# Two layers of a graph network on one core: layer 0 issued in rounds written out by hand, over four tiles at different stages

## Chip, cores and metric

The kernel runs on one core of a Trainium2 chip. The metric is device time in microseconds (us), median of the runs shown. A core has TensorE (PE; its weight loads, PEld, are listed apart), VectorE (DVE), ScalarE (ACT), GpSimd (POOL) and SyncE (SP). All DMAs of this kernel are issued from SP's queue. ACT evaluates its functions from tables that are loaded in sets by an instruction of its own (ACT_TABLE_LOAD).

## The reference

3327 nodes, 128 features, a dense 0/1 adjacency matrix. Layer 0 is attention by cosine, layer 1 attention with eight channels in each of 128 slices, both with a residual and a layer norm.

```python
# layer 0
norm2 = jnp.linalg.norm(x, axis=1, keepdims=True)
cos = beta[0] * (x @ x.T) / (norm2 @ norm2.T + 1e-07)
masked = cos + (1.0 - adj) * -1000000000.0
P = jax.nn.softmax(masked, axis=1)
x = _layernorm(x + P @ x)
# layer 1
q = (x @ Wq.T).reshape(d, n, h)          # k, v alike; d = 128, h = 8
a = jnp.einsum('dnh,dmh->dnm', q, k) * scale
a = a + adj + adj
a = jax.nn.softmax(a, axis=2)
out = jnp.einsum('dnm,dmh->dnh', a, v).reshape(n, h * d)
x = _layernorm(x + out @ Wo.T)
```

## The kernel before, in words

The nodes are padded to 3328 = 26 tiles of 128. Four stages follow one another: layer 0 (with the projections to q, k and v), a pass over DRAM that turns q and k and lays out v, the attention of layer 1, and the last projection with its layer norm.

**Layer 0** takes the tiles one by one in a loop over t. Tile t holds the nodes p*26+t, one on each partition p. For each tile:

- `load_adj` brings 128 rows of the adjacency matrix into `raw` (1.66 MB), two buffers.
- `turn_adj` turns these rows on PE, four blocks of 128x128 at a time into the PSUM tile `tp` (two buffers, seven chunks), and ACT copies them as bf16 into `aT` (L242). Three tiles share one `aT`, which goes to DRAM for layer 1.
- `inverse` gives 1/(norm_q*norm_k+1e-7): on ACT a logarithm (L252) and an exponential of its negative (L253), on POOL the denominator (L255) and its product with that first value (L258), on DVE one Newton step (L259). The product goes into the buffer `s`, of which there are two, and which the scores then use.
- `scores0`: POOL turns `raw` into the mask (L264); in four pieces of 832 columns PE makes the products and DVE scales them (L267), adds the mask and keeps the minimum (L270); ACT takes the exponential and its sum (L281).
- `values0` turns these weights on PE, copies each chunk to SBUF (`pt`, on DVE and ACT by turns, L155 and L153), multiplies by x (L291), and normalises (L295 to L312): the root is exp(-0.5*ln(var)) on ACT (L306, L307), refined on DVE (L309 to L311).
- `project` turns the new row block x1 (L318) and multiplies by the three weight matrices in halves of 512 columns (L326); the copies out are on DVE and ACT (L328, L155, L153), and a DMA takes each row block to DRAM.

x1 stays in SBUF until the last stage. In this stage the order on each engine is the scheduler's: the text gives loop order, and the scheduler moves instructions within what the data allow. The call that loads the common table set for exp and log (L232) is an instruction like the others.

**The attention stage** is issued by hand: inside `tc.manual_schedule` the order on PE, ACT, DVE and POOL is that of the text. It goes over blocks of three tiles and 32 units a block, 26 steps a unit. `load_adj_tile` (L443) brings a piece of the turned adjacency for the next block, and `exp_adj_tile` takes its exponential five steps later.

**The last stage** loads the outputs row block by row block, turns and projects them, adds x1 (L823) and normalises.

Of the kernel before, what the change touches and what calls it, by code (L numbers as in the profile page):

```python
# [10 lines left out]
F32 = mybir.dt.float32  # L11
# [35 lines left out]
def gnn_two_layers(  # L47
# [24 lines left out]
    x1 = const.tile([P, T, D], F32, name="x1")  # L72
# [11 lines left out]
    aT_s = dram.tile([NB, P, T, QT * P], BF16, name="aT_s")  # L84
# [86 lines left out]

    with ExitStack() as l0:
        big = l0.enter_context(tc.tile_pool(name="l0_big", bufs=1))
        adj_raw = l0.enter_context(tc.tile_pool(name="adj_raw", bufs=2))
        adj_tp = l0.enter_context(tc.tile_pool(name="adj_tp", bufs=1))
        work = l0.enter_context(tc.tile_pool(name="l0_work", bufs=2))
        ptp = l0.enter_context(tc.tile_pool(name="l0_pt", bufs=3))
        ps_sc = l0.enter_context(tc.tile_pool(name="l0_sc", bufs=2, space=PSUM))
        ps_tp = l0.enter_context(tc.tile_pool(name="l0_tp", bufs=2, space=PSUM))
        ps_x = l0.enter_context(tc.tile_pool(name="l0_x", bufs=2, space=PSUM))  # L180

        xs = big.tile([P, T, D], F32, name="xs")
        nc.gpsimd.memset(xs[:, T - 1, :], 0.0)
        xf = xs.rearrange("p t d -> p (t d)")
        for part, width in node_parts():
            nc.sync.dma_start(xf[part, :width], node_blocks(x, part, width))
        nbeta = const.tile([P, 1], F32, name="nbeta")
        nc.sync.dma_start(nbeta, bass.AP(tensor=beta.tensor, offset=beta.offset, ap=[[0, P], [1, 1]]))
        nc.vector.tensor_scalar_mul(nbeta, nbeta, -1.0)
        ones = const.tile([P, P], F32, name="ones")  # L190
        nc.gpsimd.memset(ones, 1.0)

        tiny = const.tile([P, 1], F32, name="tiny")
        nc.gpsimd.memset(tiny, 1e-7 * 2.0**-20)
        back = const.tile([P, 1], F32, name="back")
        nc.gpsimd.memset(back, -20.0 * math.log(2.0))

        raws = {0: load_adj(adj_raw, 0)}
        ws = []
        for name, w in (("wq", wqT), ("wk", wkT), ("wv", wvT)):  # L200
            wt = big.tile([P, C], F32, name=name)
            nc.sync.dma_start(wt, w)
            ws.append(wt)

        xT = big.tile([P, NP], F32, name="xT")
        for c in range(NCH):
            tp, a, b = turn(ps_tp, lambda t: xs[:, t, :], c)
            copy(c, xT.rearrange("r (p t) -> r t p", t=T)[:, a:b, :], tp)


        sq = work.tile([P, NP], F32, name="s")
        nc.gpsimd.tensor_mul(sq, xf, xf)
        norm_q = const.tile([P, T], F32, name="norm_q")
        nc.vector.reduce_sum(norm_q, sq.rearrange("p (t d) -> p t d", t=T), axis=AX.X)
        nc.scalar.activation(norm_q, norm_q, AF.Sqrt)
        norm_s = const.tile([P, T], F32, name="norm_s")
        nc.vector.tensor_scalar_mul(norm_s, norm_q, 2.0**-20)
        sqT = work.tile([P, NP], F32, name="s")
        nc.vector.tensor_mul(sqT, xT, xT)
        norm_k = big.tile([P, NP], F32, name="norm_k")  # L220
# [9 lines left out]
        for j in range(NPC):  # L230
            nc.scalar.activation(piece(norm_k, j), score_piece(ones, sqT, j), AF.Sqrt)
        nc.scalar.preload_act_table_set("natural_log_exp_and_others")  # L232

        def turn_adj(t: int, raw):

            b, i = divmod(t, QT)
            if i == 0:
                turn_adj.aT = adj_tp.tile([P, T, QT * P], BF16, name="aT")
            aT = turn_adj.aT
            for c in range(NCH):  # L240
                tp, k0, k1 = turn(ps_tp, lambda k: every(raw, k), c)
                nc.scalar.copy(aT[:, k0:k1, i * P : (i + 1) * P], tp)  # L242
            if i == QT - 1:
                nc.sync.dma_start(aT_s[b], aT)
            elif t == T - 1:
                w = (i + 1) * P
                nc.sync.dma_start(aT_s[b][:, :, :w], aT[:, :, :w])

        def inverse(t: int):

            y = work.tile([P, NP], F32, name="y")
            nc.scalar.activation(y, norm_k, AF.Ln, bias=tiny, scale=norm_s[:, t : t + 1])  # L252
            nc.scalar.activation(y, y, AF.Exp, bias=back, scale=-1.0)  # L253
            s = work.tile([P, NP], F32, name="s")
            nc.gpsimd.tensor_scalar(  # L255
                s, norm_k, norm_q[:, t : t + 1], 1e-7, op0=ALU.mult, op1=ALU.add
            )
            nc.gpsimd.tensor_mul(s, s, y)  # L258
            nc.vector.scalar_tensor_tensor(y, s, -2.0, y, op0=ALU.add, op1=ALU.mult)  # L259
            return s, y  # L260

        def scores0(t: int, raw, s, y):
            mn = small.tile([P, NPC], F32, name="mn")
            nc.gpsimd.tensor_scalar(raw, raw, -1.0, 1.0e9, op0=ALU.add, op1=ALU.mult)  # L264
            for j in range(NPC):
                sc = score_piece(every(xT, t), xT, j)
                nc.vector.scalar_tensor_tensor(  # L267
                    piece(s, j), sc, nbeta, piece(y, j), op0=ALU.mult, op1=ALU.mult
                )
                nc.vector.tensor_tensor_reduce(  # L270
                    out=piece(s, j),
                    in0=piece(s, j),
                    in1=piece(raw, j),
                    scale=-1.0,
                    scalar=BIG if j == 0 else mn[:, j - 1 : j],
                    op0=ALU.add,
                    op1=ALU.min,
                    accum_out=mn[:, j : j + 1],
                )
            den = small.tile([P, 1], F32, name="den0")  # L280
            nc.scalar.activation(s, s, AF.Exp, bias=mn[:, NPC - 1 : NPC], scale=-1.0, accum_out=den)  # L281
            return den

        def values0(t: int, s, den):
            acc = ps_x.tile([P, 512], F32, name="px")[:, :D]
            for c in range(NCH):
                tp, k0, k1 = turn(ps_tp, lambda k: every(s, k), c)
                pt = ptp.tile([P, 4, P], F32, name="pt")[:, : k1 - k0, :]
                copy(c, pt, tp)
                for k in range(k0, k1):  # L290
                    nc.tensor.matmul(  # L291
                        acc, pt[:, k - k0, :], xs[:, k, :], start=(k == 0), stop=(k == T - 1)
                    )
            rden = small.tile([P, 1], F32, name="rden0")
            nc.vector.reciprocal(rden, den)  # L295
            hid = small.tile([P, D], F32, name="hid")
            nc.vector.scalar_tensor_tensor(hid, acc, rden, xs[:, t, :], op0=ALU.mult, op1=ALU.add)

            stats = small.tile([P, nc.vector.BN_STATS_DIM], F32, name="stats0")
            mv = small.tile([P, nc.vector.BN_AGGR_DIM], F32, name="mv0")  # L300
            nc.vector.bn_stats(stats, hid)
            nc.vector.bn_aggr(mv, stats)
            var = small.tile([P, 1], F32, name="var0")
            nc.vector.tensor_scalar(var, mv[:, 1:2], EPS, None, op0=ALU.add)
            r = small.tile([P, 1], F32, name="r0")
            nc.scalar.activation(r, var, AF.Ln)  # L306
            nc.scalar.activation(r, r, AF.Exp, scale=-0.5)  # L307
            u = small.tile([P, 1], F32, name="u0")
            nc.vector.scalar_tensor_tensor(u, r, var, r, op0=ALU.mult, op1=ALU.mult)  # L309
            nc.vector.tensor_scalar(u, u, -0.5, 1.5, op0=ALU.mult, op1=ALU.add)  # L310
            nc.vector.tensor_mul(r, r, u)  # L311
            nc.vector.tensor_scalar(  # L312
                x1[:, t, :], hid, mv[:, 0:1], r, op0=ALU.subtract, op1=ALU.mult
            )

        def project(t: int):
            tp = ps_x.tile([P, 512], F32, name="px")
            nc.tensor.transpose(tp[:, :P], x1[:, t, :], ident)  # L318
            x1T = ptp.tile([P, P], F32, name="x1T")
            nc.scalar.copy(x1T, tp[:, :P])  # L320
            for n, (wt, dst) in enumerate(zip(ws, (q_s, k_s, v_s))):
                row = ptp.tile([P, C], F32, name="row")
                for i in range(2):
                    pq = ps_x.tile([P, 512], F32, name="px")
                    half = slice(i * 512, (i + 1) * 512)
                    nc.tensor.matmul(pq, x1T, wt[:, half], start=True, stop=True)  # L326
                    if n == 0:
                        nc.vector.tensor_scalar_mul(row[:, half], pq, float(D) ** -0.5)  # L328
                    else:
                        copy(i, row[:, half], pq)  # L330
# [536 lines left out]
```

## Time and profile before

| What | us |
|---|---|
| Median of 3 runs | 16244.1 (16243.56 to 16246.24) |
| The profiled execution | 16240.19 |
| Its span, first to last instruction | 16238.4 |
| PE busy in the span | 15584.8 (96%) |
| DVE busy | 13924.8 (86%) |
| ACT busy | 12722.5 (78%) |
| POOL busy | 13962.9 (86%) |

The profile is of one execution. "Busy" counts time in which an engine has an instruction in work; a row of the groups reads line, engine, operation, output<-inputs with shapes, count, then busy us, mean ns of one, and the idle time before them with what ended it. In the timeline the columns are start, duration, engine, line, operation, and in brackets the idle time before it and its releaser. The granted PE clock is a share of the full clock. TensorE's fp32 matmuls appear as two records each, its transposes as one.

### The profile page before, as it was taken

To read this page: it belongs to the slowest core of one execution; us is meant where nothing else is said; L and a number is where in the kernel's file an instruction comes from. 1 tells how busy PE (TensorE), PEld (TensorE's weight loads), DVE (VectorE), ACT (ScalarE), POOL (GpSimd) and SP (SyncE) were. 2 spreads that over 40 slices of the span, in tenths; PEclk is the share of its full clock that TensorE was granted. 3 is DMA by queue.
4 is the path that set the end of the run, shared out by engine and by line. 5 is a ranking of instruction groups with operands and counts; after the bars stand their busy time and mean duration, and the time that the engine had idled before them with its cause. 6 is when DMAs were issued, how large, how long until landed. Compare 5 with 4: busy or idle time off the path is not lost.

```text
span 16238.4 us, 506936 instructions
## 1 busy us (share of the span) xinstructions
PE 15584.8 (96%) x217532; PEld 7003.8 (43%) x217532; DVE 13924.8 (86%) x16184; ACT 12722.5 (78%) x24850; POOL 13962.9 (86%) x9107
## 2 busy tenths in 40 slices
PE   6765999999999999999999999999999999999999
PEld 5542444444444444444444444444444444444555
DVE  5545999999999999999999999999999999998775
ACT  5533888888888888888888888888888888888776
POOL 3334999999999999999999999999999999998886
PEclk7776999999999999999999999999999999999999
DMA  2245111111111111111111111111111111111112
GB/s 101 100 169 213 50 44 50 56 50 48 46 56 50 50 46 53 51 50 50 44 56 50 50 50 51 50 50 50 55 46 50 50 56 46 48 50 59 60 60 70
DMA packets 415024, 988.90 MB, mean 61 GB/s; under 512 B 192224, under 2 KB 312544, under 8 KB 367200
## 3 DMA queue, kind: packets, MB, share of 16 engines
q1 hardware_dynamic: 412768, 956.46, 17.1%
q8 instruction: 1704, 27.92, 0.7%
q14 instruction: 552, 4.52, 0.1%
HBM read 808.05 MB, written 148.24 MB: 59 GB/s over the span
## 4 chain that ended last, share of the span: by engine, by line
PE 89%; DVE 2%; issue 0%; ACT 0%; DMA 0%; SPq 0%; POOL 0%; ACTq 0%; POOLq 0%; DVEq 0%
PE acc L625 28%; PE ea L595 20%; PE m L516 15%; PE eb L608 12%; PE ea L608 9%; PE ea L614 2%; PE eb L614 2%; DVE mx L531 1%; PE ea L581 1%; PE ea L643 1%; DVE mx L552 1%; PE pp L822 0%; ACT pa L770 0%; DVE oT L155 0%; DMA vt_s<-vals 0%
## 5 line engine op out<-in xcount | busy, mean ns | idle before, releaser
L741 POOL TENSOR_TENSOR pb<-pb,eT 128x768 f32<-128x768 f32 (+1 forms) x7488 | 13182.9, 1766 | 1090.6 <-ACT pb L740 815.4
L531 DVE TENSOR_REDUCE mx<-m 128x2 f32<-128x1024 f32 x6784 | 8277.8, 1220 | 512.4 <-PE eb L614 214.0
L740 ACT ACTIVATE pb<-eb 128x768 f32<-128x768 f32 (+1 forms) x7488 | 5901.6, 788 | 2498.1 <-PE eb L614 1639.2
L516 PE MATMUL m<-kx,qx 32*128 32x512 f32 (+1 forms) x23296 | 6767.6, 470 | 71.6 <-DVE mx L531 40.2
L770 ACT ACTIVATE pa<-ea 128x384 f32<-128x384 f32 (+1 forms) x14976 | 6336.2, 477 | 51.0 <-PE ea L595 38.9
L625 PE MATMUL acc<-pb,vt 128*9 128x384 f32 (+1 forms) x29952 | 5903.1, 474 | 0.1
L625 PE MATMUL acc<-pa,vt 128*9 128x384 f32 (+1 forms) x29952 | 5900.3, 474 | 0.0
L552 DVE TENSOR_REDUCE mx<-m 128x1 f32<-128x512 f32 x6400 | 4382.6, 685 | 682.4 <-PE m L516 317.9
L608 PEld LDWEIGHTS <-one 3*128 3x128 bf16 x29952 | 1519.0, 91 | 5537.6 <-issue 4656.5
L595 PE MATMUL ea<-aT,two 128*32 128x384 bf16 (+1 forms) x59904 | 3715.0, 325 | 0.0
L614 PE MATMUL ea<-qx,kx 32*128 32x384 f32 (+1 forms) x14976 | 3458.8, 437 | 0.0
L614 PE MATMUL eb<-qx,kx 32*128 32x384 f32 (+1 forms) x14976 | 3443.1, 451 | 0.0
L608 PE MATMUL ea<-cx,one 3*128 3x384 bf16 (+1 forms) x14976 | 3309.0, 322 | 1.2
L516 PEld LDWEIGHTS m<-kx,qx 32*128 32x128 f32 x23296 | 2814.7, 182 | 453.4 <-DVE mx L531 95.4
L608 PE MATMUL eb<-cx,one 3*128 3x384 bf16 (+1 forms) x14976 | 2464.1, 326 | 9.7 <-ACT pb L740 8.9
L625 PEld LDWEIGHTS acc<-pa,vt 128*9 128x9 f32 x29952 | 1410.4, 91 | 788.5 <-issue 0.3
L595 PEld LDWEIGHTS <-two 128*32 128x32 bf16 x59904 | 945.5, 95 | 1418.6 <-issue 1278.1
L614 PEld LDWEIGHTS eb<-qx,kx 32*128 32x128 f32 x14976 | 1461.9, 189 | 0.0
L614 PEld LDWEIGHTS ea<-qx,kx 32*128 32x128 f32 x14976 | 1434.9, 182 | 7.4 <-issue 2.5
L625 PEld LDWEIGHTS acc<-pb,vt 128*9 128x9 f32 x29952 | 1415.4, 91 | 0.6 <-POOL pb L741 0.6
L556 DVE TENSOR_REDUCE mx<-m 128x2 f32<-128x512 f32 x1088 | 748.5, 688 | 95.3 <-PE eb L614 37.6
L542 DVE TENSOR_REDUCE mx<-m 128x4 f32<-128x1024 f32 x288 | 351.8, 1222 | 26.8 <-PE m L516 25.4
(128 smaller groups left out, 5154.1 us busy)
## 6 DMA issues: line engine op xcount, KB each, us to landing
kx<-kp_s SPq DMA_DIRECT2D x576, 832.0 KB, 4.7
vt<-vt_s SPq DMA_DIRECT2D x288, 468.0 KB, 4.9
qx<-qp_s SPq DMA_DIRECT2D x1024, 48.0 KB, 5.1
raw<-in_adj_dram SPq DMA_DIRECT2D x25, 1663.5 KB, 6.2
aT_s<-aT SPq DMA_DIRECT2D x8, 2496.0 KB, 7.4
aT<-aT_s SPq DMA_DIRECT2D x208, 96.0 KB, 2.0
vt_s<-vals SPq DMA_DIRECT2D x8, 1872.0 KB, 17.7
q_s<-row SPq DMA_DIRECT2D x26, 512.0 KB, 2.6
```

The lines of the kernel that those rows point to most:

```text
L516: nc.tensor.matmul(dst, u.qx[rows(a), q * P : (q + 1) * P], u.kx[rows(a), k0:k1], start=True, stop=True,)
L531: nc.vector.tensor_reduce(u.mx[:, h, qs[0], c], m, axis=AX.X, op=ALU.max)
L542: nc.vector.tensor_reduce(dst, m.rearrange("p a (x k) -> p a x k", x=2), axis=AX.X, op=ALU.max)
L552: nc.vector.tensor_reduce(u.mx[:, a, qs[0], c : c + 1], m, axis=AX.X, op=ALU.max)
L556: nc.vector.tensor_reduce(u.mx[:, a, qs[0] : qs[1] + 1, c], m.rearrange("p (q k) -> p q k", q=2), axis=AX.X, op=ALU.max,)
L595: nc.tensor.matmul(e[r, : u.nq], two[:, r], aT[:, j, : u.nq], start=False, stop=True, tile_position=(0, 32 * c), skip_group_check=True,)
L608: nc.tensor.matmul(e[:, : u.nq], one[r], u.cx[r, : u.nq], start=True, stop=False, skip_group_check=True)
L614: nc.tensor.matmul(e[:, : u.nq], u.kx[rows(a), j * P : (j + 1) * P], u.qx[rows(a), : u.nq], start=False, stop=stop, skip_group_check=True,)
L625: nc.tensor.matmul(acc[32 * h : 32 * h + H + 1, : u.nq], u.vt[:, h, j], pts[h // 2][:, h % 2, : u.nq], start=(j == 0), stop=(j == T - 1), ...
L740: nc.scalar.activation(pt_b[:, :, : u.nq], e_b[:, :, : u.nq], AF.Exp)
L741: nc.gpsimd.tensor_tensor(pt_b[:, :, : u.nq], pt_b[:, :, : u.nq], eT[:, j, : u.nq].unsqueeze(1).to_broadcast([P, 2, u.nq]), ALU.mult,)
L770: nc.scalar.activation(pt_a[:, h, : u.nq], e[:, : u.nq], AF.Exp)
```

## The change

Layer 0 is written as rounds inside `tc.manual_schedule`. In round t, for t from -1 to 27, tile t+1 has its adjacency turned, its mask made and its inverse norms computed, tile t its scores, tile t-1 its weights and values, and tile t-2 its norm and projections; each round has eight steps k. Further:

- The inverse uses ln(norm_k + 1e-7/norm_q) with 1/norm_q folded into the scale of the scores; product and Newton step are both on DVE, the product in a buffer `n` of its own.
- x is loaded twice, once by tiles of the strided kind and once in natural order (`xn`), and the weights are turned in natural order.
- All projection copies are on ACT; `raw` has three buffers, `aT` one, `acc0` and `pq` in PSUM one each.
- The weights' exponential is taken in two halves with two sums.
- x1 goes to DRAM tile by tile and is read back in the last stage; the turned adjacency is stored tile by tile, and attention reads it in rows of 128 instead of 384.

The diff, cut to its core (functions that only changed name or place are left out):

```diff
-    x1 = const.tile([P, T, D], F32, name="x1")
-    aT_s = dram.tile([NB, P, T, QT * P], BF16, name="aT_s")
+    aT_s = dram.tile([T, P, T, P], BF16, name="aT_s")
+    x1_s = dram.tile([T, P, D], F32, name="x1_s")
...
-        adj_raw = l0.enter_context(tc.tile_pool(name="adj_raw", bufs=2))
+        adj_raw = l0.enter_context(tc.tile_pool(name="adj_raw", bufs=3))
...
-        ps_x = l0.enter_context(tc.tile_pool(name="l0_x", bufs=2, space=PSUM))
+        ps_x = l0.enter_context(tc.tile_pool(name="l0_x", bufs=1, space=PSUM))
...
+        def adj_chunk(t: int, c: int):
+            u = tiles[t]
+            if c == 0:
+                u.aT = ptp.tile([P, T, P], BF16, name="aT", bufs=1)
+            tp, a, b = turn(ps_tp, lambda k: every(u.raw, k), c)
+            nc.scalar.copy(u.aT[:, a:b, :], tp)
+            if c == NCH - 1:
+                nc.sync.dma_start(aT_s[t], u.aT)
...
+            nc.scalar.activation(u.y, norm_k, AF.Ln, bias=norm_c[:, t : t + 1])
...
+            nc.scalar.activation(tiles[t].y, tiles[t].y, AF.Exp, scale=-1.0)
...
+            u.n = one_n.tile([P, NP], F32, name="n")
+            nc.vector.scalar_tensor_tensor(
+                u.n, norm_k, norm_c[:, t : t + 1], u.y, op0=ALU.add, op1=ALU.mult
+            )
...
+            nc.vector.scalar_tensor_tensor(u.y, u.n, -2.0, u.y, op0=ALU.add, op1=ALU.mult)
...
+            part = u.s[:, i * half : (i + 1) * half]
+            nc.scalar.activation(
+                part, part, AF.Exp, bias=u.mn[:, NPC - 1 : NPC], scale=-1.0,
+                accum_out=u.den[:, i : i + 1],
+            )
...
+            tp, a, b = turn(ps_tp, lambda k: u.s[:, k * P : (k + 1) * P], c)
+            u.pts[c] = ptp.tile([P, 4, P], F32, name="pt")[:, : b - a, :], a, b
+            copy(c, u.pts[c][0], tp)
...
+        def norm_end(t: int):
+            u = tiles[t]
+            w = small.tile([P, 1], F32, name="w0")
+            nc.vector.tensor_mul(w, u.r, u.r)
+            nc.vector.tensor_mul(w, w, u.var)
+            nc.vector.tensor_scalar(w, w, -0.5, 1.5, op0=ALU.mult, op1=ALU.add)
+            nc.vector.tensor_mul(u.r, u.r, w)
...
+            nc.sync.dma_start(x1_s[t], u.x1)
...
+            pq = ps_x.tile([P, 512], F32, name="pq")
+            nc.tensor.matmul(pq, u.x1T, ws[n][:, cols], start=True, stop=True)
+            nc.scalar.activation(
+                u.row[:, cols], pq, AF.Copy, scale=float(D) ** -0.5 if n == 0 else 1.0
+            )
...
+            for j in range(NPC):
+                nc.scalar.activation(piece(norm_k, j), score_piece(ones, sqT, j), AF.Sqrt)
+            nc.scalar.preload_act_table_set("natural_log_exp_and_others")
+
+            for t in range(-1, T + 2):
...
+                for k in range(8):
+                    if k == 0 and there(t + 2) and t > 0:
+                        load(t + 2)
+                    if k == 0 and there(t - 2):
+                        norm_begin(t - 2)
+                    if k == 0 and there(t - 1):
+                        weights(t - 1, 0)
+                        weights(t - 1, 1)
+                    if k == 1 and there(t - 2):
+                        norm_root(t - 2)
+                    if there(t) and k in (0, 2, 4, 6):
+                        scores(t, k // 2)
+                    if k == 2 and there(t - 2):
+                        norm_end(t - 2)
+                    if k < NCH and there(t + 1):
+                        adj_chunk(t + 1, k)
+                    if k == 1 and there(t + 1):
+                        inverse_log(t + 1)
+                    if k == 2 and there(t + 1):
+                        inverse_exp(t + 1)
+                    if k > 0 and there(t - 1):
+                        turn_weights(t - 1, k - 1)
+                        if k > 1:
+                            weigh0(t - 1, k - 2)
+                    if k == 3 and there(t - 2):
+                        project_turn(t - 2)
+                    if there(t - 2):
+                        for i in {4: (0,), 5: (1, 2), 6: (3,), 7: (4, 5)}.get(k, ()):
+                            project(t - 2, i)
+                    if k == 6 and there(t + 1):
+                        mask(t + 1)
+                    if k == 7 and there(t + 1):
+                        inverse_product(t + 1)
+                        inverse_newton(t + 1)
+                if there(t - 1):
+                    weigh0(t - 1, NCH - 1)
...
-            nc.sync.dma_start(aT[:, j, :w], aT_s[b][:, j, :w])
+            nc.sync.dma_start(
+                aT[:, j, :w].rearrange("p (q n) -> p q n", n=P),
+                aT_s[b * QT : b * QT + w // P, :, j].rearrange("q p n -> p q n"),
+            )
...
+            x1 = work.tile([P, D], F32, name="x1r")
+            nc.sync.dma_start(x1, x1_s[t])
...
-            nc.vector.tensor_add(hid[:, t, :], pp, x1[:, t, :])
+            nc.vector.tensor_add(hid[:, t, :], pp, x1)
```

In the prediction, A, W and S with a number stand for the adjacency chunk, the weight chunk and the score piece of that number (adj_chunk, turn_weights, scores).

## The prediction

> **What bounds the kernel now.** I read the stages first. Busy time of each engine in four stretches (layer 0, the pass that turns q, k and v, attention, the last stage), columns: length, PE, PE weight load, DVE, ACT, POOL, granted PE clock, DMA share, GB/s:
>
> ```profile
> 38.00:1112.00 1074.00, 757.29 (x3426) 579.93 (x3424) 581.83 (x780) 548.64 (x588) 380.80 (x102) 0.79 0.25 97
> 1112.00:1410.00 298.00, 81.28 (x416) 73.13 (x416) 71.20 (x121) 59.58 (x113) 82.30 (x64) 0.59 1.03 374
> 1410.00:16122.00 14712.00, 14647.08 (x212976) 6263.92 (x212976) 13219.67 (x15140) 12082.07 (x24102) 13488.25 (x8927) 1.00 0.15 51
> ```
>
> Attention is 91% of the span, with PE full, and is edited only in how it loads the mask. In layer 0 no engine is full and DMA is idle three quarters of the time: waiting, not work, sets its length. So the stake is layer 0's 1074 us. Second view: the timeline of one tile; it repeats every 40.96 us (L258 starts at 558.90 and 599.85).
>
> ```profile
> 558.90 7.21 POOL L258 TENSOR_TENSOR s<-s,y 128x3328 f32<-128x3328 f32 x1
> 562.28 3.84 DVE L309 SCALAR_TENSOR_TENSOR u<-r,var 128x1 f32<-128x1 f32 x1 [3.50 <-ACT r L307]
> 566.80 3.62 DVE L259 SCALAR_TENSOR_TENSOR y<-s,y 128x3328 f32<-128x3328 f32 x1
> 568.79 4.45 POOL L264 TENSOR_SCALAR raw<-raw 128x3328 f32<-128x3328 f32 x1 [2.68 <-PE tp L165]
> 585.03 3.07 ACT L281 ACTIVATE s<-s,mn 128x3328 f32<-128x3328 f32 x1
> 596.73 3.04 POOL L255 TENSOR_SCALAR s<-norm_k,norm_q 128x3328 f32<-128x3328 f32 x1 [13.38 <-PE tp L165]
> 599.85 7.21 POOL L258 TENSOR_TENSOR s<-s,y 128x3328 f32<-128x3328 f32 x1
> ```
>
> It is one ring: POOL makes the product (10.3 us, L255 and L258), DVE the Newton step and the scores (566.8 to 584), ACT the exponential, PE turns the weights, and only when the last chunk of s is turned may POOL reuse the buffer (13.38 us of waiting). Two lines show a lock: L309, a 128x1 operation, takes 3.84 us because it ends with POOL's L258, and L264 takes 4.45 where alone (at 30.14) it took 2.96. Third view, groups of layer 0 on ACT: four table loads in a tile (L252 and L281 have 24 more each).
>
> ```profile
> L306 ACT ACT_TABLE_LOAD x26 | 33.4, 1283 | 0.5
> L307 ACT ACT_TABLE_LOAD x26 | 33.4, 1283 | 0.5
> ```
>
> **The change, part by part.** Costs are from these rows. Work per tile:
> - PE is unchanged: 26+26 transposes at 0.135 (eight in 1.08 us), 16 score records at 0.35 (starts 30.23, 30.58), 52 value records at 0.1125 (twelve in 1.60, sixteen in 2.05), 12 projection records at 0.43 (starts 573.44, 573.87), together 23.7 us at full clock.
> - POOL loses L255 and L258; only the mask stays (2.96).
> - DVE gets the product (priced as L259, 3.62), keeps Newton (3.62), four scores (1.08+1.11), four copies (2.5) and the norm (2.5), and loses the projection copies: 21 us.
> - ACT loses four loads (5.1), gets four more projection copies (0.59 each): log 3.07, two exponentials (2.97, and 3.5 in halves), adjacency copies 3.6, projection 3.8, weights 1.7, root 0.4: 19 us.
>
> No engine's work exceeds 24 us, but the new order is fixed on each engine, so I walk one full round. The ring that I find runs from the end of one Newton step (DVE, last in a round) to the next:
> 1. norm_begin stands next on DVE (1.5 with sums and gaps, as 598.65 to 599.73 shows); norm_root on ACT waits for it (0.1+0.4); behind it stand adjacency copy 1 (0.6), the log (3.1), copy 2 (0.6), the exponential (3.0) and weight copy 1 (0.6). Sum 10.0.
> 2. There are two tp buffers, and weight turn 2 needs the one that copy 1 frees. From there PE issues in order: turn 0.54, values 0.9, S2 1.4, A4 0.54, W3 0.54, values 0.9, projection 0.86, A5 0.54, W4 0.54, values 0.9, projection 0.86, a wait of 0.9 for the single pq buffer, projection 0.86, S3 1.4, x1 turn 0.14. Sum 11.8.
> 3. DVE: score 3 (0.25+1.08). The mask starts on POOL after the last adjacency turn, 0.5 after S3, and by the lock rows holds off the reduction, which reads s and raw from SBUF: until 3.5, then 1.2; copy 0.45; product and Newton 7.24. Sum 12.4.
>
> 34.2 us at full PE clock. Ahead of step 2 PE has only 4.5 us of work in 13 (longest gap 3.1). What that does to the clock is the main choice. Stretches of 3.41 us, cut where the clock steps:
>
> ```profile
> 558.67:562.08 3.41, 1.22 (x8) 1.03 (x8) 0.11 (x1) 3.35 (x6) 3.33 (x2) 1.00 0.00 0
> 562.08:565.49 3.41, 1.12 (x4) 0.72 (x4) 3.21 (x1) 1.72 (x4) 3.41 (x1) 0.50 0.00 0
> 565.49:568.93 3.44, 1.99 (x8) 1.89 (x9) 3.33 (x5) 0.89 (x3) 0.76 (x2) 0.50 0.00 0
> 568.93:572.34 3.41, 3.41 (x7) 1.34 (x6) 2.38 (x3) 0.23 (x1) 3.41 (x1) 0.50 0.00 0
> 572.34:575.75 3.41, 3.41 (x14) 2.22 (x14) 3.17 (x6) 0.59 (x1) 0.90 (x1) 1.00 0.39 154
> ```
>
> PE fell to half after a window with 1.22 us busy, stayed there over one with 1.99, and rose after a full one. The Trainium skill (TensorE: Matmul & The Clock Gate, What's actually happening) asks for an idle window of about 3.4 us before the clock falls; by it the 3.1 us gap is harmless, P = 34.2 and the forecast 16079. By the rows, 35% busy is enough to fall. I take the rows: the rise comes 3.41 to 6.83 us after the dense part begins, mean 5.1, in which half the work is lost: 2.6. Bounds: 0, and the whole dense part at half (10.9). **P = 36.8 us a round**, against 40.96.
>
> The rounds at the ends, same walk. Setup: x comes twice; the first copy landed at 11.3, I put the second at 17 (a raw tile of that size lands in 6.2 us); square 5.7 and sum 3.6 (L212, L214), small steps 1.2, xT copies 3.5, squares of columns on POOL 4 behind them, last scores, Sqrt 2.3: 38, as now. First Newton ends 19.4 later with the mask behind it, second 19.0, third (no norm yet) 28.1: 66.5. Then 23 rounds. After the last Newton: drain of scores 18.4, weights, values, projection 21, last norm and six projections through one buffer 17: 56. End of layer 0: 38 + 66.5 + 23x36.8 + 56 = 1007, against 1112: 105 us less.
>
> Costed at nothing:
> - The mask loads of attention fall into pieces of 256 B instead of 768, three times the packets for 234 transfers that land in 2.0 us; they are asked for five steps ahead, 9.8 us (14712/7488 = 1.96 a step). Without that cover a landing 1 us too late costs up to 1 us each; below nothing there is no gain, PE is full.
> - Adjacency stores now go out per tile (852 KB; 2.5 MB took 7.4) into one aT buffer; 9 us pass before the next round's first copy. If late, ACT waits there, behind it the root and the log.
> - SP gets x1 stores and xr loads, some eight issues of 0.32 in a round. In the last stage 26 x1 loads of 0.32 stand between row loads; PE sets its pace (3.36 a tile, rows land in 3.3 with three buffers): 0, at most 8 us.
> - The shorter chain of norm_end (no lock) lies beside PE.
>
> The profiled execution is 16240.19 (span 16238.4), 3.9 below the median 16244.1. 16244.1 - 105 = **16139**.
>
> **Rivals.** A is the above.
>
> B, the clock stays up or the mask slips in without blocking: P 31 to 34.5, 16006 to 16086. For: each is one term of 2 to 2.6 us. Against: the window and lock rows.
>
> C, PE-bound rounds: if the tp waits do not bind (other slots), P is 23.7 plus some 2 of pq waits; 38+66.5+23x26+56 = 758, so 15890. For: engine sums. Against: log and exponential stand whole in ACT's order between copies that PE needs.
>
> D, it doesn't do what it says: the load of the common set at L232 ran at 0.74, ahead of the Sqrt loads, so before it was undone. If loads still come before root, log and exponential, four stand in step 1: by the rows 5.1 us, P = 41.9, end 1124, 16256. The skill (ScalarE: Activation LUTs, What ACT_TABLE_LOAD costs) adds a drain to each, 2.66 in all: P = 47.4, and 16383; the rows show the next ACTIVATE 1.29 after a load's start, so I take 5.1. Against: the new order puts the load behind the last Sqrt.
>
> E, slower: PE never gets a full window. The same page (Part 4: PE-mode transpose) says transposes don't count as busy for the gate; a quarter of the dense part is transposes. Then PE stays at half: 47.4 us of work a round, P = 47.4, with the ends some 20 longer 1273, 16405. It decides from P = 41.4 ((1112-160.5)/23), which is two thirds of the dense part at half. Against: in the last stage eight transposes and sixteen matmuls alternate every 3.36 us and the clock stays at 1.00; and at half speed PE has fewer gaps.
>
> **How the numbers follow.** A 0.50, B 0.24, C 0.08, D 0.08, E 0.10. A alone (P 35 to 39.5) gives 16098 to 16201. The range 16010 to 16260 takes in A, B and D and leaves C and E out. Measurement can tell 0.2% (32 us) from no change: faster is A, B, C, 0.82; same D, 0.08; slower E, 0.10.
>
> **What would show it.** Right: rounds of 36 to 38 us; no table load between tiles; ACT's root waiting on DVE; PE idle about 3 us before weight turn 2, with 0.50 clock there; a reduction of some 3 us after S3 where the mask runs; attention still 14712. Wrong: rounds under 34 or over 40, a longer attention stage, or weight turn 2 not waiting for the exponential.

## The result, and the profile after

| | us |
|---|---|
| Before, median of 4 runs | 16243.8 |
| After, median of 4 runs | 16094.2 (16091.67 to 16094.52) |
| Ratio | 0.9907, 95% interval 0.989 to 0.9925 |
| The profiled execution after, and its span | 16094.0, 16092.2 |

The changed kernel is 150 us faster; 105 were forecast. First the stages, in the view that opened the prediction (columns: length, PE, PE weight load, DVE, ACT, POOL, granted PE clock, DMA share, GB/s):

```profile
44.00:955.00 911.00, 687.09 (x3452) 520.85 (x3450) 573.82 (x754) 478.02 (x652) 81.17 (x51) 0.93 0.32 116
955.00:1253.00 298.00, 81.23 (x416) 73.59 (x416) 70.81 (x121) 59.25 (x113) 82.39 (x64) 0.60 1.02 374
1253.00:15977.00 14724.00, 14657.61 (x212976) 6259.40 (x212976) 13214.21 (x15140) 12076.65 (x24103) 13487.40 (x8927) 1.00 0.15 51
```

Layer 0 ends at 955.3 instead of 1112.2: all of the gain, and a little more, for attention runs from its first product to its last copy in 14714.6 where before took 14702.7. In layer 0 POOL has become idle (81 us), the clock has gone from 0.79 to 0.93, and PE is still a quarter idle. From the end of setup on, ACT's groups of layer 0 hold one table load where there were four in every tile:

```profile
L404 ACT ACT_TABLE_LOAD x1 | 1.3, 1283 | 0.0
```

One round, from the timeline, in order of time (start, duration, engine, line, operation; idle time before and its releaser in brackets). It repeats every 34.13 us, which 478.84 and 512.97 show:

```profile
478.84 3.63 DVE L242 SCALAR_TENSOR_TENSOR y<-n,y 128x3328 f32<-128x3328 f32 x1
...
483.95 0.20 ACT L310 ACTIVATE r<-var 128x1 f32<-128x1 f32 x1 [2.60 <-DVE var L304]
...
484.76 3.07 ACT L228 ACTIVATE y<-norm_k,norm_c 128x3328 f32<-128x3328 f32 x1
...
488.20 2.99 ACT L231 ACTIVATE y<-y 128x3328 f32<-128x3328 f32 x1
491.08 0.58 ACT L154 COPY pt<-tp 128x512 f32<-128x512 f32 x1
...
491.71 1.12 PE L166 MATMUL tp<-ident,s 128*128 128x128 f32 x4 [2.62 <-ACT pt L154]
...
503.27 1.56 PE L190 MATMUL sc<-xT 128*128 128x416 f32 x4
504.87 1.08 DVE L250 SCALAR_TENSOR_TENSOR s<-sc,by_q,y 128x832 f32<-128x832 f32 x1 [4.27 <-PE sc L190]
505.14 2.98 POOL L221 TENSOR_SCALAR raw<-raw 128x3328 f32<-128x3328 f32 x1 [30.05 <-PE tp L166]
505.99 3.00 DVE L253 CUSTOM_DVE_ANT_0 s<-s,raw,mn 128x832 f32<-128x832 f32 x1
...
509.26 3.67 DVE L236 SCALAR_TENSOR_TENSOR n<-norm_k,norm_c,y 128x3328 f32<-128x3328 f32 x1
512.97 3.63 DVE L242 SCALAR_TENSOR_TENSOR y<-n,y 128x3328 f32<-128x3328 f32 x1
```

This is the forecast's ring, station by station: Newton ends at 482.47; the norm follows on DVE and the root on ACT waits for it (2.60); log and exponential stand whole ahead of the weight copy; W2 waits for that copy (2.62); the order of PE leads to S3; DVE waits for S3 (4.27); the last reduction takes 3.00 beside POOL's mask, where its three brothers in the round take 1.02 to 1.09; product and Newton close the round.

The clock. Every change of the granted clock in this trace lies on a grid of 3.413 us; these are four stretches of that grid (columns as above):

```profile
484.75:488.17 3.42, 2.16 (x16) 1.89 (x16) 3.25 (x6) 3.42 (x3) 0.00 (x0) 1.00 0.00 0
488.17:491.58 3.41, 0.84 (x6) 0.54 (x4) 1.52 (x7) 3.41 (x4) 0.00 (x0) 1.00 0.07 22
491.58:494.99 3.41, 3.28 (x14) 3.18 (x15) 0.69 (x1) 0.77 (x3) 0.00 (x0) 0.50 0.02 5
494.99:498.41 3.42, 3.42 (x22) 2.79 (x21) 2.00 (x2) 1.14 (x3) 0.00 (x0) 1.00 0.00 0
```

Behind a stretch with 2.16 us of PE work the clock stays, behind one with 0.84 it falls, and the next one, with 3.28, brings it back. Each round has one half-clock stretch with 3.28 us of work in it, and half of that work's time, 1.64 us, is lost.

### The profile page after: what moved, and what is told of

Same layout as the page of the kernel before. It is cut to its first block, busy times and chain, and to the rows that moved or that the text cites. A ratio compares the mean times of both kernels' runs of the same rounds, so it can differ in the third digit from the quotient of the medians.

```text
span 16092.2 us, 507025 instructions
## 1 busy us (share of the span) xinstructions
PE 15517.9 (96%) x217532; PEld 6935.5 (43%) x217532; DVE 13906.8 (86%) x16159; ACT 12637.3 (79%) x24904; POOL 13664.8 (85%) x9062
## 4 chain that ended last, share of the span: by engine, by line
PE 92%; DVE 4%; ACT 2%; DMA 1%; issue 1%; POOL 0%; SPq 0%; DVEq 0%; POOLq 0%; ACTq 0%
PE acc L725 28%; PE ea L695 20%; PE m L616 15%; PE eb L708 12%; PE ea L708 9%; PE ea L714 2%; PE eb L714 2%; DVE mx L631 1%; PE ea L681 1%; PE tp L166 1%; PE ea L743 1%; PE acc L288 1%; DVE y L242 1%; DVE n L236 1%; PE pq L342 1%
## 5 line engine op out<-in xcount | busy, mean ns | idle before, releaser
L221 POOL TENSOR_SCALAR raw<-raw 128x3328 f32<-128x3328 f32 x26 | 78.6, 3022 | 738.7 <-PE tp L166 727.9
```

## The experiments

All are compared with the kernel before on the same chip, where it took 16240.2 to 16243.7. "Round" or "tile" is the mean time between two Newton steps in the middle of layer 0.

### The ring of the written order, taken apart

**mask_early** moves the last adjacency turn and the mask one step earlier, so that the mask no longer starts behind the last score piece, where it meets that piece's reduction.

```diff
-                    if k < NCH and there(t + 1):
-                        adj_chunk(t + 1, k)
+                    if k < NCH - 1 and there(t + 1):
+                        adj_chunk(t + 1, k)
+                    if k == NCH - 2 and there(t + 1):
+                        adj_chunk(t + 1, k + 1)
...
-                    if k == 6 and there(t + 1):
+                    if k == 5 and there(t + 1):
                         mask(t + 1)
```

> The last adjacency chunk is turned one step earlier (k=5), and the mask stands at k=5, so that POOL has finished it before DVE's last reduction. Ring theory: that reduction falls from 3.00 to 1.08 us and the round shortens by 1.9 us. How much of it shows depends on the clock. If delays simply add: period 32.2, 23 rounds make 44 us. If the round stays tied to the 3.413 us grid on which the clock changes (before: 40.96 = 12 of them, after: 34.13 = 10), it goes to 30.72 = 9 of them (78 us less) or stays at 34.13. Rival, that PE's work or something else sets the round: no change, within 5 us.

16063.2; a round of 33.0, none of the lengths expected. Rounds of 31.97, 33.52 and 33.53 follow one another, together 99.0: 29 stretches of the clock's grid. All reductions are short again, and POOL's mask now lies beside a wait and a copy of DVE:

```profile
516.79 2.97 POOL L221 TENSOR_SCALAR raw<-raw 128x3328 f32<-128x3328 f32 x1 [23.50 <-PE tp L166]
517.19 0.65 PE L166 MATMUL tp<-ident,s 128*128 128x128 f32 x4 [0.48 <-ACT aT L215]
517.88 0.69 DVE L156 COPY pt<-tp 128x512 f32<-128x512 f32 x1 [2.25 <-PE tp L166]
523.96 1.08 DVE L253 CUSTOM_DVE_ANT_0 s<-s,raw,mn 128x832 f32<-128x832 f32 x1
```

Of the 1.9 us that the reduction lost to the mask, a round without a fall of the clock wins only 0.7 (31.97 here, 32.65 in pe_kept_busy below): an ACT copy of the moved turn now stands in front of a weight turn (0.48), and DVE waits longer for the next one (2.25, where it was 1.32). The lock is real; most of its price had been cover for other waits.

**copy1_on_dve** takes the weight copy of chunk 1 from ACT, where log and exponential stand ahead of it, to DVE.

```diff
-            copy(c, u.pts[c][0], tp)
+            copy(0 if c == 1 else c, u.pts[c][0], tp)
```

> Weight copy 1 goes from ACT, where it stands behind the exponential, to DVE. Ring theory: weight turn 2 no longer waits for the exponential and starts some 2.2 us earlier; period 31.9 by simple addition (51 us less in 23 rounds), 30.3 to 30.7 if PE's gap then becomes too short for the clock to fall. Rival, that the wait before weight turn 2 is not on the ring: period 34.13 as before, and PE idles elsewhere.

16038.7; most rounds 31.43, the mean 31.65. W2 waits less and for another engine:

```profile
494.31 0.66 PE L166 MATMUL tp<-ident,s 128*128 128x128 f32 x4 [1.40 <-DVE pt L156]
```

So the ring does pass through log, exponential and that copy. W2 starts 8.0 us behind the Newton step instead of 9.2: the shorter wait is 1.2 of the 2.5 us. The other 1.3 are put down to the clock: most rounds now have no half-clock stretch, or have it while PE waits for W2, and take 31.43 all the same.

**pe_kept_busy** puts two products without a use (128x512) ahead of W2, where PE waits.

```diff
+                    if k == 3 and there(t - 2):
+                        for _ in range(2):
+                            warm = ps_x.tile([P, 512], F32, name="pq")
+                            nc.tensor.matmul(warm, ident, xT[:, :512], start=True, stop=True)
                     if k > 0 and there(t - 1):
                         turn_weights(t - 1, k - 1)
```

> Two idle products of 128x512 (4 records, 1.72 us, result unused) stand on PE in its 2.7 us gap before weight turn 2. Clock theory: the window that now has 0.84 of 3.41 us busy rises to 2.6, the clock does not fall, the 1.6 us lost at half clock are gone: period 32.5, 37 us less, although PE has more to do. Rival, that the half-clock window lies beside the ring or that the round is tied to the grid whatever the clock does: 34.13, no change. If the idle products delay the turn: longer.

16059.3: work was added, and the kernel became 35 us faster. Rounds take 32.65, 33.07 and 33.17 by turns, mean 32.93. In the shortest the clock doesn't fall:

```profile
442.81 2.21 PE L434 MATMUL pq<-xT,ident 128*128 128x512 f32 x4
445.60 0.66 PE L166 MATMUL tp<-ident,s 128*128 128x128 f32 x4 [0.58 <-ACT pt L154]
```

W2 waits for the same copy here and starts 9.25 us behind the Newton step, as in the changed kernel (9.24). So the clock alone makes the difference: 34.13 - 32.65 = 1.5, beside the 1.64 read off the half-clock stretch. In the other two rounds of three the clock still falls, because the grid cuts the round elsewhere, ahead of the idle products:

```profile
503.84:507.25 3.41, 1.65 (x12) 1.46 (x13) 3.28 (x5) 3.41 (x3) 0.00 (x0) 1.00 0.06 17
507.25:510.67 3.42, 3.42 (x12) 2.05 (x10) 1.99 (x8) 3.42 (x4) 0.00 (x0) 0.50 0.06 19
```

The idle products then run in part at half clock, and W2 starts some 0.5 us later.

**ring_delay** adds a memset on DVE to each round, between the last weight copy and the product.

```diff
                     if k == 7 and there(t + 1):
+                        nc.vector.memset(idle[:, :300], 0.0)
                         inverse_product(t + 1)
```

> A memset of 128x300 on DVE (about 0.3 us) stands ahead of the product in each round, on the ring. If delays add: period 34.43, 7 to 8 us more. If the round is tied to the 3.413 us grid: the half-clock window takes it up, period 34.13 as before and the time within 3 us, with weight turn 2 starting some 0.3 to 0.6 us later after the clock's fall.

```profile
491.22:494.63 3.41, 2.90 (x14) 2.90 (x15) 0.69 (x1) 0.95 (x2) 0.00 (x0) 0.50 0.02 5
```

```profile
491.74 1.12 PE L166 MATMUL tp<-ident,s 128*128 128x128 f32 x4 [2.62 <-ACT pt L154]
...
509.18 0.31 DVE L444 MEMSET idle<- 128x300 f32 x1
```

16091.9, a round of 34.14: the memset cost nothing. From the start of the last weight copy to that of Newton it adds 0.20 us (4.24 for 4.04), which in 26 rounds would be 5. The round is ten stretches of the clock's grid (10 x 3.413 = 34.13). W2, and with it the dense part, starts 0.52 us after its half-clock stretch does, where it was 0.13. So 2.90 us of work run at half speed instead of 3.28, 1.45 us are lost instead of 1.64, and that gives the delay back. The kernel before fits the same: 40.96 = 12 x 3.413.

**three_moves** joins the first two edits and moves two projections later.

```diff
-                        for i in {4: (0,), 5: (1, 2), 6: (3,), 7: (4, 5)}.get(k, ()):
+                        for i in {4: (0,), 5: (1,), 6: (2,), 7: (3, 4, 5)}.get(k, ()):
```

> The early mask and the weight copy on DVE together, and the projections moved so that only one stands between two score pieces (one each at k = 4, 5, 6, three at k = 7), which takes a projection and a wait for its buffer, 1.76 us, out of PE's part of the ring. Ring theory: 31.43 - 0.7 - 1.76 = 29.0 us a round at full clock, up to 1.7 more where the clock falls; 78 to 118 us less than the changed kernel, 15975 to 16015. Rival, that PE's order at the end of the round (three projections through one buffer) or ACT becomes the bound: 30.5 to 31.5.

15978.1 (0.9836, 0.982 to 0.9852); every round between 29.14 and 29.17, beside 29.0 worked out, and no half-clock stretch from the fourth Newton step to the last. The model of the ring holds, and the clock's loss and the lock to its grid go with the gap.

### Which part of the change carries the gain

**one_table**: the kernel before, with the square roots of layer 0's setup as exp(0.5*ln), so that no other function comes between log and exponential and the scheduler leaves no load between tiles.

```diff
-            nc.scalar.activation(piece(norm_k, j), score_piece(ones, sqT, j), AF.Sqrt)
+            nc.scalar.activation(piece(norm_k, j), score_piece(ones, sqT, j), AF.Ln, bias=tiny)
+            nc.scalar.activation(piece(norm_k, j), piece(norm_k, j), AF.Exp, scale=0.5)
```

(norm_q alike.)

> The kernel before with one part of the change alone: its two Sqrt of the setup are written as exp(ln/2), so that the common table set, loaded at the start, stays. All 26x4 table loads between tiles should be gone. If all their time counts: 5.1 us a tile, 133 us less, which would be nearly the whole gain of the change. Ring theory of the kernel before: only the load ahead of the weights' exponential (1.28 us) lies on its ring, the root's two lie beside POOL's product and the logarithm's waits for DVE anyway: 33 us less if it adds, 0 if the tile stays tied to twelve steps of 3.413 us (40.96), 89 if it falls to eleven (37.55).

16183.3 (0.9966, 0.995 to 0.9981), 60 us faster: none of the numbers expected. A tile takes 38.7 instead of 40.96, by turns 37.8, 37.9 and 40.3, together 34 stretches of 3.413. Loads of 5.1 us per tile gave 2.3.

**rows_of_384**: the changed kernel with the turned adjacency stored and read in rows of 384 as before.

```diff
-                nc.sync.dma_start(aT_s[t], u.aT)
+                b, i = divmod(t, QT)
+                nc.sync.dma_start(aT_s[b][:, :, i * P : (i + 1) * P], u.aT)
...
+            nc.sync.dma_start(aT[:, j, :w], aT_s[b][:, j, :w])
```

> The changed kernel with the turned adjacency in the old layout (rows of 384 for attention, written by tile in pieces of 256 B). Attention grew by 12 us (14702.7 to 14714.6, and 14709 to 14714 in the variants). If the small pieces of the mask loads are the cause: attention back to 14703, 12 us less. Rival, that it is spread over all units and has nothing to do with the loads: 14709 to 14715 as before.

16093.3; attention takes 14710.4 against 14714.6. The pieces of 256 B are at most 4 of the 12 us, and perhaps none: mask_early, which has them, takes 14709.0.

**scheduler_order**: the changed kernel without `tc.manual_schedule` around layer 0, so that the scheduler orders the same operations; Sqrt as in one_table, so that no load comes back.

```diff
-        with tc.manual_schedule(engines={...}):
+        if True:
```

> The changed kernel without the hand-written order in layer 0: the same functions in the same text, order left to the scheduler; the Sqrt of the setup as exp(ln/2), so that the table set stays in both. If the hand order carries the gain: 37 us or more a round and a total above 16150. Rival, that the parts (no table loads, product on DVE in its own buffer, no lock on the root) carry it and the order little: 33 to 35 us a round, 16070 to 16110.

15845.3 (0.9754, 0.9735 to 0.9774): 249 us faster than the changed kernel. My theory, that the written order carries the gain, fell, and so did its rival. Layer 0 from 300 to 500 us, first of the changed kernel:

```profile
300.00:500.00 200.00, 151.46 (x785) 117.11 (x785) 131.49 (x174) 108.61 (x148) 18.40 (x12) 0.95 0.35 126
```

then of this one:

```profile
300.00:500.00 200.00, 190.80 (x1069) 149.93 (x1069) 169.89 (x229) 143.94 (x202) 25.13 (x16) 1.00 0.47 171
```

PE is busy 95% of the time at full clock. The order repeats every six tiles, and a tile takes 24.8 us on average (the expectations that follow reckon with 23.9): 23.7 of them are PE's own work, as the forecast had counted it. The same operations in the written order take 34.1.

**scheduler_sqrt**: the same with Sqrt and preload as the change has them.

> The changed kernel with its operations as they are, its Sqrt and its table preload included, but layer 0 left to the scheduler's order instead of the order written out. The scheduler is free to put the preload ahead of the Sqrt of setup, and then nothing keeps log and exponential in one table: four loads of 1.28 us would stand on ACT for every tile, as in the kernel before. In the scheduler-order run ACT is busy 19.2 us of the 23.9 of a tile, and PE 23.7. Theory 1: with the order free, table loads go into ACT's spare time for the most part: ACT then holds 19.2 + 5.1 = 24.3 us per tile, just above PE's 23.7, and a tile takes 24.3 to 26: 15855 to 15905. Theory 2: each load delays a copy that PE waits for, the full 5.1 per tile: 27 x 5.1 = 138 more, about 15983. If the loads do not come back (0 table loads between tiles), it is a repetition of that run at 15845 with the Sqrt form undone.

15957.4 (0.9824, 0.9808 to 0.9841). Loads are back between tiles, some four in a tile (groups of ACT, 300 to 500 us, two of five):

```profile
L310 ACT ACT_TABLE_LOAD x7 | 9.0, 1283 | 0.1
L228 ACT ACT_TABLE_LOAD x7 | 9.0, 1283 | 0.1
```

112 us more than scheduler_order, 112/26 = 4.3 per tile, of the 5.1 that four loads last: nearer to theory 2. (A tile takes 29.5; where an expectation below has 30.2 - 23.9 = 6.3 for the loads, 29.5 - 24.8 = 4.7 is measured.) This run differs from the changed kernel in nothing but who sets the order, and is 137 us faster even with the loads. It also says that the preload keeps its place, and the one table set its use, only through the written order or by doing without Sqrt.

**old_loop_two_parts**: the kernel before, its loop, its buffers and its x1 in SBUF, with one_table's edit and this one:

```diff
-            s = work.tile([P, NP], F32, name="s")
+            n = big.tile([P, NP], F32, name="n")
             nc.gpsimd.tensor_scalar(
-                s, norm_k, norm_q[:, t : t + 1], 1e-7, op0=ALU.mult, op1=ALU.add
+                n, norm_k, norm_q[:, t : t + 1], 1e-7, op0=ALU.mult, op1=ALU.add
             )
-            nc.gpsimd.tensor_mul(s, s, y)
-            nc.vector.scalar_tensor_tensor(y, s, -2.0, y, op0=ALU.add, op1=ALU.mult)
+            nc.vector.tensor_mul(n, n, y)
+            nc.vector.scalar_tensor_tensor(y, n, -2.0, y, op0=ALU.add, op1=ALU.mult)
+            s = work.tile([P, NP], F32, name="s")
```

> The kernel before with two parts of the change alone: layer 0's square roots as exp(ln/2), so that one table set serves (38.6 us per tile by itself, 16183), and the product of the quotient moved from POOL to DVE into a buffer of its own, n, in place of the score buffer s. All else stays: the old loop, the scheduler's order, x1 in SBUF, two adjacency buffers. Theory 1: the ring through the two s buffers (the product of tile t+1 cannot start before the weights of tile t-1 are turned) and POOL's product hold the rest of the old period; without them a tile comes near PE's own work, 25 to 29 us: 26 x (38.6 - 27) = 300 less, about 15880 (15830 to 15935). Theory 2: the rest of the old period lies elsewhere (the adjacency buffers, the projection's shared PSUM), and a tile still takes 34 or more: above 16060.

15845.9 (0.9756, 0.9742 to 0.9771), 24.2 us per tile: theory 1, and level with the best, from two small edits. Timeline of one tile:

```profile
473.59 3.06 POOL L257 TENSOR_SCALAR n<-norm_k,norm_q 128x3328 f32<-128x3328 f32 x1 [8.48 <-DVE y L261]
...
489.59 3.62 DVE L260 TENSOR_TENSOR n<-n,y 128x3328 f32<-128x3328 f32 x1
...
494.07 3.60 DVE L261 SCALAR_TENSOR_TENSOR y<-n,y 128x3328 f32<-128x3328 f32 x1
```

The sum on POOL, which in the kernel before waited 13.38 us for PE to turn the old weights out of `s`, now starts when Newton has left `n` (its releaser is DVE's y) and is done 13 us before the product wants it. The ring that held the tile is open, and the same stretch shows PE full:

```profile
300.00:500.00 200.00, 196.00 (x1110) 158.58 (x1110) 180.14 (x255) 130.81 (x155) 51.12 (x25) 1.00 0.47 176
```

**product_alone**: the last diff without the table edit.

> The kernel before with one part of the change alone: the product of the quotient on DVE into a buffer of its own, n, its sum left on POOL; the Sqrt and the table loads stay as before (four of 1.28 us per tile). Beside the kernel before (40.96 us per tile), the run with the tables alone (38.6) and the run with both (24.0) it completes the square. Theory 1: the buffer and the product carry nearly all of it and the loads cost what they cost in the scheduler-order layer with the Sqrt left in, 30.2 - 23.9 = 6.3 per tile: 30 to 30.5 per tile, 26 x (40.96 - 30.2) = 280 less than before, about 15960 (15940 to 15985). Theory 2: neither part does much alone (the loads stand in ACT's order between the copies that PE needs, and the ring only closes up when both are gone): 35 or more per tile, above 16085.

15926.6 (0.9808, 0.9791 to 0.9824); every tile 27.23, better than either theory's number. It completes a square, in us per tile:

| | product on POOL, in `s` | product on DVE, in `n` |
|---|---|---|
| four table loads per tile | 40.96 | 27.23 |
| none | 38.7 | 24.2 |

The product's move is worth 13.7 to 14.5 us a tile, the tables 2.3 to 3.0. New buffer and new engine were changed together; no run separates them.

**x1_resident**: scheduler_order with x1 kept in SBUF and neither stored nor read back.

```diff
-            u.x1 = ptp.tile([P, D], F32, name="x1")
+            u.x1 = x1[:, t, :]
...
-            nc.sync.dma_start(x1_s[t], u.x1)
```

> The scheduler-order version with layer 0's output kept in SBUF for the whole kernel as before the change, no store to DRAM and no load in the last stage. Theory 1: the 12 us that the attention stage has grown come with the output's move (another place of the attention's buffers in SBUF); with it undone the stage takes 14703 again and the time is 10 to 14 below 15845: 15831 to 15835. Theory 2: the move costs and saves nothing, 15843 to 15848, and the 12 us come from elsewhere.

15844.0 (0.9754, 0.974 to 0.9769), attention 14709.3: theory 2. The output's move to DRAM costs and saves nothing that can be measured.

## Why the prediction was right, and where its terms were off

Its sign, its range and its ring held; its main number was 45 us too high. Of the signs that it named, four came: one table load, the root waiting on DVE, PE idle ahead of W2, and the long reduction. The half clock came not in that wait, as said there, but from 0.13 us ahead of W2 on. The rounds missed the 36 to 38 us and stayed just over the 34 that would have spoken against it. A longer attention stage, which it named as a sign of being wrong, came too, by 12 us.

- **The period**, 36.8 forecast, 34.13 measured, is the large term: 23 x 2.67 = 61 us. Step 1 (norm, root, log, exponential, copy) took 482.47 to 491.71, 9.2 against 10.0 (its terms add up to 9.9). Step 2 (PE to S3) took 13.2 until DVE could go on, 11.5 without the clock's 1.64, against 11.8. Step 3 took 11.7 against 12.4. The clock took 1.64, not 2.6: the rise was placed 5.1 us into the dense part on average, but the start of that part is not spread over the grid. The round locks to it, and W2 starts 0.13 us after the stretch does.
- **The rule and the row.** Without a clock loss the prediction had P = 34.2, 16079. The measured 34.13 looks like it, but that is luck: the clock does fall in every round, and the ring without it is 32.5, as pe_kept_busy's rounds of 32.65 show. The row was the right one to follow: a stretch with 0.84 us of work is not idle, and the clock fell behind it. What the Trainium skill says on the same page (TensorE: Matmul & The Clock Gate, What's actually happening), that the window is free-running, is what the lock rests on, and the traces agree: in each of them every change of clock lies on one grid of 3.413.
- **The ends.** Setup's last Sqrt ended at 44.2, not 38, and the first Newton at 62.9; by the third the rounds of the start had made most of that good (106.4 against 104.5). From the last Newton to the last copy took 63.3, not 56. Together 9 us against the forecast; I have not taken the drain apart.
- **Costed at nothing.** Stores of x1, loads of xr and the last stage (115.6 against 116.4) did cost nothing. Attention lost 12 us. The smaller pieces were named and bounded there, but rows_of_384 gives only 4 back and x1_resident, against scheduler_order, 3. The stage took 14702.1 in old_loop_two_parts and 14715.1 in three_moves, and 14704.9 in scheduler_sqrt, which has the new layout. What moves it by up to 0.1% stays open.
- **Rivals.** D fell: one load. E fell: full stretches bring the clock back, and transposes count as work. The pass behind layer 0 shows that, for PE does nothing but transposes in it (the last section has the lines); the trace before shows the same at 1125 to 1132 us, so E could have been set aside from it. E's "same page" is TensorE's, not the one that D names; what it says of transposes did not hold here. The result lies between B's upper end (16086) and A's lower (16098), and for A's reason. C was set aside because log and exponential stand whole in ACT's order between copies that PE needs. That is true of the written order and of nothing else: with the same operations in the scheduler's order a tile takes 24.8 and the kernel 15845, near C's 15890. The prediction read the order as the change's strength and asked only what the ring costs; the experiments show that the order gives back 9.3 of the 16.1 us per tile that the other edits win (40.96 to 24.8).

## What to carry to other kernels

When no engine is full, look for the buffer that closes the ring before writing an order: here one buffer of its own and one product on another engine gave 13.7 us of a tile's 41, inside the old loop. An order written out by hand can make rings of its own, as here where a long instruction stands ahead of a short one that another engine waits for; compare it with the scheduler's order of the same operations before tuning it. And where half-clock stretches recur once a round, small changes of the ring may show nothing, since the round can sit on the clock's grid.

## What the runs showed of the hardware

- In each trace the changes of the granted clock lie 3.413 us apart or multiples of it, and loops with a half-clock stretch in every round lock to the grid: 40.96 (12), 34.13 (10), one_table's three tiles (34). A memset of 0.31 us added to such a round cost nothing; added PE work made it 1.2 us shorter. Loops without a half-clock stretch are not on the grid (29.16, 24.18).
- A stretch need not be idle for the clock to fall behind it: it fell behind stretches with 0.84 and 1.65 us of PE work, and stayed behind one with 2.16.
- A DVE reduction with two SBUF operands takes 3.00 us instead of 1.08 when POOL starts a 128x3328 operation ahead of it; it ends 0.87 us behind POOL's. A copy out of PSUM that starts 1.1 us into the same mask (mask_early, 517.88) takes its usual 0.69.
- Transposes alone bring the clock back. In the changed kernel's pass behind layer 0 (960 to 1250 us), PE's only instructions are 416 transposes. A stretch full of them follows one without PE work, both at half clock, and the next has the full clock:

```profile
L166 PE MATMUL tp<-ident,by_t 128*128 128x128 f32 x416 | 81.2, 377 | 199.8 <-POOL by_t L458 189.5 <-DVE low L470 10.1
```

```profile
1017.24:1020.65 3.41, 3.41 (x16) 3.41 (x17) 1.38 (x2) 1.72 (x3) 1.49 (x1) 0.50 0.73 186
1020.65:1024.06 3.41, 1.29 (x12) 1.05 (x10) 3.11 (x6) 1.88 (x5) 1.70 (x3) 1.00 1.11 341
```
